# Output matmuls of each batch as narrow, wide, wide, narrow, and another order of the last two batches in a graph-attention kernel

## The chip, the cores and the metric

One core of a Trainium2 chip runs the kernel. The metric is the device time of one launch in microseconds (us); lower is better. The engines are named as the profile names them: PE (TensorE matmul) with PEld (its weight load), DVE (VectorE), ACT (ScalarE), POOL (GpSimd) and SP (SyncE, which here only issues DMAs).

## The reference

For each of 16 batches there are 512 nodes with 512 features, a condition vector and an integer label array; all is float32. The input biases that the reference draws as zeros are given small random values here.

```python
self_feat = concat(v, q) @ W_self.T + b_self           # 512 x 512 a batch
output = self_feat
for d in range(2):                                     # two edge directions
    A = adj if d == 0 else swap(adj)                   # 512 x 20 neighbours x 11 labels
    vb = A[:, :, :20] @ w_bias + b_bias
    qh, kh = self_feat @ Wq[d].T + bq[d], kv @ Wk[d].T + bk[d]     # kv: first 20 nodes; 16 heads of 32
    aff = einsum('bnhd,bmhd->bnhm', qh, kh) / sqrt(32)
    aff = where(A.sum(-1) > 0, aff, -9e15) + vb        # the same for every head
    w = softmax(aff)                                   # over the 20 neighbours
    output += per-head projection of (w @ kv) + bout[d]
return v + relu(output)
```

## The kernel before

The features lie on partitions (four groups of 128), the 512 nodes of a batch along the free axis. After a setup stage that folds the weights, 16 batches run in a software pipeline. The order of all steps is written out by hand: the string `order` lists the steps of one period with a batch offset each, and every engine takes its instructions in that order, so an instruction whose input is late holds up all that stands behind it on its engine. One period has seven products `f1` to `f7` of the self features (`feature_product`, L286), seven products `P1` to `P7` of the scores (`score_product`, L422) and one output step, `attend` (L514). The softmax of the two directions and 16 heads is done in four units (i, l), where i is the node half within a group and l the half of the partition axis: subtract the maximum (DVE, L473), exponential (ACT, L477), sum and reciprocal (DVE, L481 and L482), multiply (POOL, L486), and transpose in 32 x 32 blocks into the tile `wt` (DVE, L492 and L493).

`attend` adds the projected neighbours to what stands in PSUM. ACT has put self feature plus bias there (`seed_out`, L505), in the banks `ps_w` (output groups 0 and 1) and `ps_e` (2 and 3). For each half c of the nodes there are two kinds of matmul, all on 32 rows of the array:

- a wide one takes a 32 x 128 weight tile and serves the last 4 neighbours of all heads: 4 a half, one for each output group q;
- a narrow one takes a 32 x 32 tile and serves the first 16 neighbours of one head: 16 a half.

Each of these is two passes in the trace (float32). Before, the order is wide c=0, wide c=1, narrow c=0, narrow c=1. After it `relu` (ACT, L532) empties the banks, `residual` (POOL, L536) adds x, and `store` (SP, L539) writes one group of 128 features.

The last batch (15) has no successor to overlap with. Its scores are four plain products (`plain_scores`, L963) in `ps_a`, `ps_u` and `ps_v`, each seeded by ACT (`seed_plain`, L952), followed by `plain_max` (DVE, L978 and L980), `plain_exp` (ACT, L984), `plain_sum` (DVE, L991 and L992), `plain_normal` (L997, on POOL, and for the last piece on DVE) and `plain_turn` (DVE, L1003 and L1004). Its output step `attend_end` (L1036) runs for c=0 in `ps_w` and `ps_e`, and for c=1 in `ps_a`, `ps_u` and `ps_v`, there in two pieces by unit. Since out = x + max(o, 0) = max(o + x, x), POOL sums self feature and x beforehand (`end_sum`, L1020), ACT seeds the banks with it (`seed_end`, L1025), and one DVE maximum with x (`end_max`, L1054) gives the result, which `end_store` (L1058) writes as four DMAs of 256 KB.

Of the kernel before, what the change touches and what calls it, by code (L numbers as in the profile page):

```python
# [13 lines left out]
P = 128  # L14
# [4 lines left out]
def gat_kernel(  # L19
# [487 lines left out]
    def attend(b):  # L507
# [10 lines left out]

        for c in range(HA):
            for q in range(HL):  # L520
                r = bass.ts(q, 32)
                mm(q, c, slice(0, P), vds[b][r, c, 1], ends[r, :, c])
        for c in range(HA):
            for e in range(HL):
                for q in range(HL):
                    r = bass.ts(q, 32)
                    mm(q, c, bass.ts(e, DH), vds[b][r, c, 0, bass.ts(e, DH)], heads[r, :, c, :, e])
# [478 lines left out]
    def end_banks(a, c):  # L1006
        if c == 0:
            return [(ps_w, ps_e)[a][:, :, :NH].rearrange("p g (x n) -> p g x n", n=32)]
        if a == 0:
            return [ps_a[:, :, :NH].rearrange("p g (x n) -> p g x n", n=32)]  # L1010
        return [t[:, :NH].rearrange("p (g x n) -> p g x n", g=1, n=32) for t in (ps_u, ps_v)]

    def end_parts(a, c, of):
        banks = end_banks(a, c)
# [7 lines left out]
    def seed_end(a, c):  # L1022
        n = a * HA + c
        for to, of in end_parts(a, c, turned(ends["sum"][:, n])):
            nc.scalar.activation(to, of, AF.Identity, bias=bo[:, n : n + 1])  # L1025

    def attend_end(c, units):
# [5 lines left out]
        def mm(q, to, lhs, rhs):  # L1033
            a, g = q // HA, q % HA
            bank = ((ps_u, ps_v)[g] if a else ps_a[:, g]) if c else (ps_w, ps_e)[a][:, g]
            nc.tensor.matmul(  # L1036
                bank[to, bass.ds(lo * P, n * P)].rearrange("p (i j n) -> p i j n", i=n, n=32),
# [11 lines left out]
    def end_max(a, c):  # L1049
        if "out" not in ends:  # L1050
            ends["out"] = load.tile([P, C, N], F32, tag="x", name="end_out", bufs=3)
        to, x = (turned(t[:, a * HA + c]) for t in (ends["out"], xs[last]))
        for (of, into), (_, of_x) in zip(end_parts(a, c, to), end_parts(a, c, x)):
            nc.vector.tensor_max(into, of, of_x)  # L1054

    def end_store(a, c, queue=nc.sync):
        n = a * HA + c
        queue.dma_start(out[last, bass.ts(n, P)], ends["out"][:, n])  # L1058

    instead = {  # L1060
        "T2": fourth_keys, "T1": lambda: full_bias(0, 0, "u1"), "T4": lambda: full_bias(1, 0, "u2"), "S1": lambda: end_sum(0),
# [3 lines left out]
    with tc.manual_schedule():  # L1065
# [33 lines left out]
        go("reluW:2 sr21:1 Lv:1 tr11:1 reluE:2 sr12:1 nm21:1 res3:2")  # L1099
# [4 lines left out]
        go("nm12:1 tr21:1 St3:2 tr12:1 res1:2 St1:2 soW:1 soE:1")  # L1104
        full_bias(0, 1, "u3")
        go("res0:2 St0:2")
        plain_max(0, 0)
        plain_exp(0, 0)
        seed_plain(0, 1)
# [99 lines left out]
```

## Time and profile before

| what | value |
|---|---|
| median of 3 runs | 557.59 us (557.59 to 558.15) |
| the profiled execution | 557.27 us, of which its span (first to last instruction) is 555.5 us |
| mean granted TensorE clock | 0.993 |
| one period of the pipeline | 28.75 us |
| first and last `attend` | at 147.1 us and 536.4 us, 15 in all |
| `attend_end` | from 543.2 us on |
| last DMA of the result is issued | at 551.15 us |

In the timelines a row has the start, the duration (for merged rows from the first start to the last end), the engine, the line, what is written and read, the shape of the weight tile (rows*columns) and of one operand, and the count; in brackets stands the idle time of the engine before the row and what ended it. A matmul's end is modelled, so times between matmuls are taken from start to start. Kernel lines in rows of before are those of the printed kernel.

### The profile page before, as it was taken

The numbers are of one execution on the slowest core, as the hardware profiler recorded it, in microseconds if no ns is written. First come the engines' busy times: TensorE is split into PE (matmuls) and PEld (weight loads), VectorE is DVE, ScalarE is ACT, GpSimd is POOL, SyncE is SP. The second block draws the span as 40 slices with busy tenths as digits, with TensorE's granted clock in tenths as the row PEclk, the third lists the DMA queues.
The fourth block names the chain that finished last, engine by engine and source line by source line (L and its number), as shares of the span: only waits on it lengthen the run. The fifth ranks groups of instructions, "written<-read, shape, count | busy, mean of one in ns | idle before, by whom it ended". The sixth has DMA issues, their size and how long they took to land.

```text
span 555.5 us, 19357 instructions
## 1 busy us (share of the span) xinstructions
PE 545.2 (98%) x8034; PEld 419.9 (76%) x8034; DVE 452.4 (81%) x726; ACT 368.8 (66%) x768; POOL 441.9 (80%) x396
## 2 busy tenths in 40 slices
PE   8999999999999999999999999999999999999994
PEld 4443446979797979797978787888888787979782
DVE  0395564699989898979898988989898989898985
ACT  1244342858686959596868686868687777866652
POOL 2235675859797979797979798988989797979695
PEclk9999999999999999999999999999999999999997
DMA  8999899996786867677686858676868676645024
GB/s 292 375 400 382 296 379 344 302 292 166 230 252 175 247 181 240 193 219 215 197 234 177 241 184 217 210 196 191 214 207 218 209 211 202 192 138 167 22 95 156
DMA packets 89336, 125.80 MB, mean 226 GB/s; under 512 B 11712, under 2 KB 56800, under 8 KB 87200
## 3 DMA queue, kind: packets, MB, share of 16 engines
q1 hardware_dynamic: 87568, 121.88, 70.6%
q0 software_dynamic: 672, 1.36, 1.0%
q8 instruction: 63, 1.03, 0.8%
q10 hardware_dynamic: 1008, 1.32, 0.7%
q14 instruction: 25, 0.20, 0.1%
HBM read 85.71 MB, written 39.19 MB: 225 GB/s over the span
## 4 chain that ended last, share of the span: by engine, by line
PE 85%; issue 4%; DMA 4%; POOL 3%; DVE 2%; SPq 1%; ACT 0%; DVEq 0%; POOLq 0%
PE ps_a L422 23%; PE ps_u L286 18%; PE ps_v L286 13%; PE ps_e L422 11%; PE ps_w L422 6%; PE ps_w L514 5%; DMA x<-in_xT 2%; PE ps_v L739 2%; DMA ws_q<-in_wsT 1%; PE ps_v L214 1%; PE ps_e L514 1%; PE ps_a L963 1%; POOL cq_d L725 1%; PE ps_u L214 1%; POOL rx L194 1%
## 5 line engine op out<-in xcount | busy, mean ns | idle before, releaser
L486 POOL TENSOR_TENSOR s<-s,sm 128x640 f32<-128x640 f32 x60 | 76.5, 1277 | 40.9 <-DVE sm L482 40.9
L343 ACT ACTIVATE prod<-adj,wb_sb 128x160 f32<-128x160 int32 x165 | 80.4, 585 | 0.3 <-DMA adj<-in_adj 0.3
L536 POOL TENSOR_TENSOR o<-o,x 128x512 f32<-128x512 f32 x60 | 77.2, 1287 | 0.0
L477 ACT ACTIVATE s<-s 128x640 f32<-128x640 f32 x60 | 42.4, 730 | 25.8 <-DVE s L473 25.8
L286 PE MATMUL ps_u<-t,ws_s 128*64 128x246 f32 x480 | 55.0, 370 | 0.0
L450 DVE TENSOR_TENSOR u<-ps_a,both 128x640 f32<-128x640 f32 x30 | 24.7, 823 | 30.1 <-PE ps_a L422 30.1
L481 DVE TENSOR_REDUCE sm<-s 128x32 f32<-128x640 f32 x60 | 47.7, 795 | 0.0
L395 POOL TENSOR_TENSOR k<-g,k 128x608 f32<-128x608 f32 x30 | 44.2, 1495 | 1.1
L405 POOL TENSOR_TENSOR s<-sf 128x512 f32<-128x512 f32 x30 | 37.8, 1280 | 7.0 <-DVE sf L316 6.1
L286 PEld LDWEIGHTS ps_u<-t,ws_s 128*64 128x64 f32 x480 | 33.9, 137 | 11.7
L492 DVE STREAM_TRANSPOSE wt<-s 128x512 f32<-128x512 f32 x60 | 41.3, 688 | 1.4 <-POOL s L486 1.3
L514 PE MATMUL ps_e<-wt,vd 32*32 32x256 f32 (+1 forms) x600 | 38.3, 388 | 0.0
L367 ACT COPY both<-add 64x160 f32<-64x160 f32 (+1 forms) x68 | 21.5, 316 | 25.2 <-DVE add L356 24.6
L514 PE MATMUL ps_w<-wt,vd 32*32 32x256 f32 (+1 forms) x600 | 38.0, 388 | 0.0
L260 POOL TENSOR_TENSOR t<-x 128x492 f32<-128x492 f32 x30 | 37.4, 1248 | 0.0
L356 DVE TENSOR_REDUCE add<-prod 128x160 f32<-128x1920 f32 (+1 forms) x17 | 34.5, 2029 | 2.6 <-POOL prod L351 2.6
L316 DVE TENSOR_TENSOR sf<-ps_v,f 128x492 f32<-128x492 f32 x45 | 30.0, 667 | 6.7 <-PE ps_v L286 5.9
L260 POOL TENSOR_TENSOR t<-x,t 128x492 f32<-128x492 f32 x30 | 34.7, 1158 | 0.2
L176 ACT ACTIVATE xn<-xn 128x512 f32<-128x512 f32 x56 | 34.5, 617 | 0.0
L422 PEld LDWEIGHTS ps_a<-g,sf 128*64 128x64 f32 x480 | 30.3, 137 | 5.6 <-issue 5.4
L348 DVE TENSOR_REDUCE cond<-adj 128x160 f32<-128x1760 int32 (+1 forms) x17 | 31.1, 1829 | 4.0 <-DMA adj<-in_adj 4.0
L422 PE MATMUL ps_a<-g,sf 128*64 128x152 f32 x480 | 34.2, 295 | 0.0
(329 smaller groups left out, 1511.4 us busy)
## 6 DMA issues: line engine op xcount, KB each, us to landing
g<-g_d SPq DMA_DIRECT2D x60, 304.0 KB, 4.8
g_d<-st SPq DMA_DIRECT2D x16, 1064.0 KB, 6.2
out_T<-o SPq DMA_DIRECT2D x60, 256.0 KB, 4.4
xn<-in_xn SPq DMA_DIRECT2D x28, 512.0 KB, 5.9
x<-in_xT SPq DMA_DIRECT2D x28, 512.0 KB, 7.2
adj<-in_adj SPq DMA_DIRECT2D x32, 440.0 KB, 4.7
vd<-bd_d SPq DMA_DIRECT2D x64, 64.0 KB, 2.0
nz<-nz_d SPq DMA_DIRECT2D x14, 256.0 KB, 7.0
```

What stands on the lines that cost most here:

```text
L260: nc.gpsimd.tensor_sub(t, one, two)
L286: nc.tensor.matmul(to[bass.ts(a, RA), bass.ts(i, HN)], lhs, x[:, k], start=(n, i, k) == (1, 0, 0), stop=k == 1, skip_group_check=True,)
L343: nc.scalar.activation(label_sums(b)[:, :, l], labels(b)[:, :, l], AF.Copy, scale=wb_sb[:, l : l + 1])
L395: op(t, one(), two())
L405: op(t, one(), two())
L422: nc.tensor.matmul(to[bass.ts(a, RA), j, :, 1:], rows[:, k, bass.ts(j, RA)], keys[:, k, a].rearrange("p (x m) -> p x m", m=ND), start=Fals ...
L477: nc.scalar.activation(t, t, AF.Exp)
L481: nc.vector.tensor_reduce(sm, rows_of(b, i, l), AX.X, ALU.add)
L486: nc.gpsimd.tensor_mul(t, t, us.pop((b, "sum", i, l)).unsqueeze(2).to_broadcast([P, 32, NG]))
L492: nc.vector.transpose(wts[b][:, i, l, : W * 4 // 5], t[:, :, :MW])
L514: nc.tensor.matmul((ps_w, ps_e)[a][to, g, bass.ts(c, NH)].rearrange("p (i j n) -> p i j n", i=2, n=32), lhs, rhs, start=False, stop=True, ...
L536: nc.gpsimd.tensor_add(t, t, xs[b][:, c])
```

## The change

It has two parts.

**The order within `attend`.** The narrow matmuls of c=0 now come first, then the wide ones of both halves, then the narrow ones of c=1. The matmuls are the same.

```diff
+        def head_run(c):
+            for e in range(HL):
+                for q in range(HL):
+                    r = bass.ts(q, 32)
+                    mm(q, c, bass.ts(e, DH), vds[b][r, c, 0, bass.ts(e, DH)], heads[r, :, c, :, e])
+
+        head_run(0)
         for c in range(HA):
             for q in range(HL):
                 r = bass.ts(q, 32)
                 mm(q, c, slice(0, P), vds[b][r, c, 1], ends[r, :, c])
-        for c in range(HA):
-            for e in range(HL):
...
+        head_run(1)
```

**The last two batches.** The last three sums of batch 14 are taken before its transposes (`sr12` ahead of `tr11`), so that POOL's last two multiplications of batch 14 stand ahead of the residual additions of batch 13. Of the four `end_sum`s two go (n = 0 and 2): `seed_end` for c=0 takes the self feature alone, and x is added at the end, for output groups 0 and 1 by ACT's relu and a POOL addition (`end_relu`, `end_add`), for groups 2 and 3 by DVE in one instruction (`end_both`). Batch 14's group with a=1, c=0 also gets relu and x in one DVE step (`out_both`). The last piece of `plain_normal` moves from DVE to POOL. The first unit of `attend_end` for c=1 is written to `ps_w` and `ps_e`, so that `ps_a`, `ps_u` and `ps_v` hold the last unit alone: 128 columns a group in place of 256. The result of the last batch leaves in six DMAs: two of 256 KB and four of 128 KB, one of the small ones last.

```diff
-    def end_banks(a, c):
+    def end_banks(a, c, i):
         if c == 0:
             return [(ps_w, ps_e)[a][:, :, :NH].rearrange("p g (x n) -> p g x n", n=32)]
+        if i == 0:
+            return [(ps_w, ps_e)[a][:, :, bass.ds(NH, P)].rearrange("p g (x n) -> p g x n", n=32)]
         if a == 0:
-            return [ps_a[:, :, :NH].rearrange("p g (x n) -> p g x n", n=32)]
...
+            return [ps_a[:, :, :P].rearrange("p g (x n) -> p g x n", n=32)]
...
+    def rectified(to, of, x):
+        for g in range(HA):
+            nc.vector.scalar_tensor_tensor(to[:, g], of[:, g], 0.0, x[:, g], ALU.max, ALU.add)
...
-        go("reluW:2 sr21:1 Lv:1 tr11:1 reluE:2 sr12:1 nm21:1 res3:2")
+        go("reluW:2 sr21:1 Lv:1 sr12:1 reluE:2 nm21:1 tr11:1")
...
-        go("nm12:1 tr21:1 St3:2 tr12:1 res1:2 St1:2 soW:1 soE:1")
+        go("nm12:1 tr21:1 tr12:1")
         full_bias(0, 1, "u3")
-        go("res0:2 St0:2")
+        go("res3:2 St3:2 soW:1 soE:1 res1:2 St1:2 res0:2 St0:2")
         plain_max(0, 0)
+        seed_plain(0, 1)
         plain_exp(0, 0)
-        seed_plain(0, 1)
...
-        plain_normal(1, 1, second, nc.vector)
+        plain_normal(1, 1, second)
         plain_turn(1, 1, second)
-        go("res1:1 St1:1 res2:1 St2:1 res3:1 St3:1")
-        attend_end(1, (0,))
         attend_end(1, (1,))
-        for c in range(HA):
-            for a in range(HA):
-                end_max(a, c)
-                end_store(a, c, nc.sync if (a, c) == (1, 1) else nc.scalar)
+        end_relu()
+        end_add()
+        for a in range(HA):
+            end_max(a, 0)
+        end_both()
+        for a in range(HA):
+            end_max(a, 1)
...
+        end_store(1, 1, bass.ts(1, NH), nc.sync)
```

How it stands on the engines, in three places. First PE, one batch's `attend` between a feature product (L286) and a score product (L422); `wt` are the transposed softmax weights, `vd` the projected neighbours; before, the wide rows (128 output partitions) and the first narrow ones:

```order
L286 MATMUL ps_v<-x_1530,ws_s 64x246 x8
L514 MATMUL ps_w<-wt_1610,vd_1699 128x256 x2
L514 MATMUL ps_e<-wt_1610,vd_1699 128x256 x2
L514 MATMUL ps_w<-wt_1610,vd_1699 128x256 x2
L514 MATMUL ps_e<-wt_1610,vd_1699 128x256 x2
L514 MATMUL ps_w<-wt_1610,vd_1699 32x256 x2
L514 MATMUL ps_e<-wt_1610,vd_1699 32x256 x2
```

After, from the last narrow rows of c=0 to the first ones of c=1:

```order
L514 MATMUL ps_w<-wt_1610,vd_1699 32x256 x2
L514 MATMUL ps_e<-wt_1610,vd_1699 32x256 x2
L514 MATMUL ps_w<-wt_1610,vd_1699 128x256 x2
L514 MATMUL ps_e<-wt_1610,vd_1699 128x256 x2
L514 MATMUL ps_w<-wt_1610,vd_1699 128x256 x2
L514 MATMUL ps_e<-wt_1610,vd_1699 128x256 x2
L514 MATMUL ps_w<-wt_1610,vd_1699 32x256 x2
L514 MATMUL ps_e<-wt_1610,vd_1699 32x256 x2
```

Before, the 32 narrow matmuls stand in one run behind the wide ones; after, 16 stand ahead of the wide ones and 16 behind. The array changes its tile shape four times a batch, with the way in and out, where it changed it three times.

Second POOL, from the multiplications of batch 14 (L486, tiles `s` and `sm`) to the first ones of batch 15 (`last`); `o` and `x_5619` are batch 13's result and input. Before:

```order
L486 TENSOR_TENSOR s_11_6668<-s_11_6668,sm_11_6757 128x640
L1020 TENSOR_TENSOR end_sum<-sf_6666,x_6367 128x512
L486 TENSOR_TENSOR s_10_6705<-s_10_6705,sm_10_6826 128x640
L536 TENSOR_TENSOR o_1_6836<-o_1_6836,x_5619 128x512
L486 TENSOR_TENSOR s_01_6728<-s_01_6728,sm_01_6839 128x640
L536 TENSOR_TENSOR o_0_6823<-o_0_6823,x_5619 128x512
L949 TENSOR_TENSOR full_6922<-cq_6502,both_6707 128x640
L536 TENSOR_TENSOR o_0_6823<-o_0_6823,x_5619 128x512
L997 TENSOR_TENSOR last_6926<-last_6926,max_6927 128x640
```

After:

```order
L486 TENSOR_TENSOR s_11_6668<-s_11_6668,sm_11_6757 128x640
L1027 TENSOR_TENSOR end_sum<-sf_6666,x_6367 128x512 x2
L486 TENSOR_TENSOR s_10_6705<-s_10_6705,sm_10_6827 128x640
L486 TENSOR_TENSOR s_01_6728<-s_01_6728,sm_01_6835 128x640
L952 TENSOR_TENSOR full_6915<-cq_6502,both_6707 128x640
L539 TENSOR_TENSOR o_1_6838<-o_1_6838,x_5619 128x512
L539 TENSOR_TENSOR o_0_6824<-o_0_6824,x_5619 128x512 x2
L1000 TENSOR_TENSOR last_6927<-last_6927,max_6928 128x640
```

No addition of batch 13 stands between batch 14's last two multiplications any more, and a second `end_sum` stands ahead of them.

Third DVE, the end of the program, from the last reciprocal of the softmax (`max` holds the sums by then) on. Before:

```order
L992 RECIPROCAL max_7087<-max_7087 128x16
L1003 STREAM_TRANSPOSE wt_6980<-last_7086 128x256
L1004 STREAM_TRANSPOSE wt_6980<-last_7086 128x64
L997 TENSOR_TENSOR last_7086<-last_7086,max_7087 128x320
L1003 STREAM_TRANSPOSE wt_6980<-last_7086 128x256
L1004 STREAM_TRANSPOSE wt_6980<-last_7086 128x64
L1054 TENSOR_TENSOR end_out<-ps_w,x_6367 128x2x8x32
L1054 TENSOR_TENSOR end_out<-ps_e,x_6367 128x2x8x32
L1054 TENSOR_TENSOR end_out<-ps_a,x_6367 128x2x8x32
L1054 TENSOR_TENSOR end_out<-ps_u,x_6367 128x8x32
L1054 TENSOR_TENSOR end_out<-ps_v,x_6367 128x8x32
```

After:

```order
L995 RECIPROCAL max_7090<-max_7090 128x16
L1006 STREAM_TRANSPOSE wt_6977<-last_7089 128x256
L1007 STREAM_TRANSPOSE wt_6977<-last_7089 128x64
L1006 STREAM_TRANSPOSE wt_6977<-last_7089 128x256
L1007 STREAM_TRANSPOSE wt_6977<-last_7089 128x64
L1072 TENSOR_TENSOR end_out<-ps_w,x_6367 128x2x4x32
L1072 TENSOR_TENSOR end_out<-ps_e,x_6367 128x2x4x32
L1063 SCALAR_TENSOR_TENSOR end_out<-ps_e,x_6367 128x8x32 x2
L1072 TENSOR_TENSOR end_out<-ps_a,x_6367 128x2x4x32
L1072 TENSOR_TENSOR end_out<-ps_u,x_6367 128x4x32
L1072 TENSOR_TENSOR end_out<-ps_v,x_6367 128x4x32
```

The multiplication L997 is gone from DVE, and the three steps that read the banks of the last matmuls have half their columns.

More of the change, by code (lines that the diff above doesn't have):

```diff
@@ L522, in attend @@
                 mm(q, c, slice(0, P), vds[b][r, c, 1], ends[r, :, c])
-        for c in range(HA):
-            for e in range(HL):
-                for q in range(HL):
-                    r = bass.ts(q, 32)
-                    mm(q, c, bass.ts(e, DH), vds[b][r, c, 0, bass.ts(e, DH)], heads[r, :, c, :, e])
+        head_run(1)
     def relu(b, a):
@@ L1020, in end_sum, with seed_end @@
         nc.gpsimd.tensor_add(ends["sum"][:, n], sfs[last][:, n], xs[last][:, n])
-    def seed_end(a, c):
+    def seed_end(a, c, i=0):
         n = a * HA + c
-        for to, of in end_parts(a, c, turned(ends["sum"][:, n])):
+        for to, of in end_parts(a, c, i, ends["sum"] if c else sfs[last]):
             nc.scalar.activation(to, of, AF.Identity, bias=bo[:, n : n + 1])
@@ L1034, in mm @@
             a, g = q // HA, q % HA
-            bank = ((ps_u, ps_v)[g] if a else ps_a[:, g]) if c else (ps_w, ps_e)[a][:, g]
+            bank = ((ps_u, ps_v)[g] if a else ps_a[:, g]) if lo else (ps_w, ps_e)[a][:, g]
             nc.tensor.matmul(
-                bank[to, bass.ds(lo * P, n * P)].rearrange("p (i j n) -> p i j n", i=n, n=32),
+                bank[to, bass.ds(NH * (c - lo), n * P)].rearrange("p (i j n) -> p i j n", i=n, n=32),
                 lhs, rhs, start=False, stop=True, skip_group_check=True,
@@ L1103, in gat_kernel @@
         plain_scores(1, 0)
-        go("nm12:1 tr21:1 St3:2 tr12:1 res1:2 St1:2 soW:1 soE:1")
+        go("nm12:1 tr21:1 tr12:1")
         full_bias(0, 1, "u3")
-        go("res0:2 St0:2")
+        go("res3:2 St3:2 soW:1 soE:1 res1:2 St1:2 res0:2 St0:2")
         plain_max(0, 0)
+        seed_plain(0, 1)
         plain_exp(0, 0)
-        seed_plain(0, 1)
+        plain_max(1, 0, first)
         plain_sum(0, 0)
         plain_normal(0, 0)
+        plain_max(1, 0, second)
+        plain_exp(1, 0)
+        plain_scores(0, 1)
         full_bias(1, 1, "u1")
-        go("res2:2 St2:2")
-        plain_max(1, 0, first)
-        plain_max(1, 0, second)
-        plain_scores(0, 1)
-        plain_exp(1, 0)
-        seed_plain(1, 1, first)
-        seed_plain(1, 1, second)
         plain_turn(0, 0)
@@ L1122, in gat_kernel @@
         plain_normal(1, 0)
-        end_sum(2)
-        end_sum(1)
+        go("res2:2 St2:2")
+        seed_plain(1, 1, first)
+        seed_plain(1, 1, second)
         go("OUT:1 Lv:0")
```

75 lines of the change are left out of this document (55 added, 20 removed).

## The prediction

> **What bounds the kernel now.** I read the page first, for the busy shares and the chain that ended last, then a table by stage over one period, then PE's timeline, then all engines at the end.
>
> ```profile
> span 555.5 us, 19357 instructions
> PE 545.2 (98%) x8034; PEld 419.9 (76%) x8034; DVE 452.4 (81%) x726; ACT 368.8 (66%) x768; POOL 441.9 (80%) x396
> PE 85%; issue 4%; DMA 4%; POOL 3%; DVE 2%; SPq 1%; ACT 0%; DVEq 0%; POOLq 0%
> ```
>
> PE is busy for 98% of the span, and 85% of the chain that ended last is PE's. A share of the span hides stages, so here is one period of the pipeline (columns: time, then busy time of PE, PEld, DVE, ACT, POOL):
>
> ```profile
> 437.19:465.94 28.75, 28.75 (x418) 23.93 (x420) 25.46 (x40) 22.00 (x46) 25.59 (x23) 1.00 0.73 210
> ```
>
> In the steady state PE never stops, at full clock (1.00), and DVE and POOL have more than 3 us of 28.75 to spare. A microsecond that PE saves in a period is a microsecond of the kernel. This is PE's timeline through one output step, starts in the first column:
>
> ```profile
> 319.62 0.48 PE L514 MATMUL ps_w<-wt,vd 32*128 32x256 f32 x2
> ...
> 319.94 0.38 PE L514 MATMUL ps_w<-wt,vd 32*128 32x256 f32 x2
> ...
> 320.37 0.38 PE L514 MATMUL ps_w<-wt,vd 32*128 32x256 f32 x2
> ...
> 320.69 0.41 PE L514 MATMUL ps_w<-wt,vd 32*32 32x256 f32 x2
> ...
> 320.93 0.38 PE L514 MATMUL ps_w<-wt,vd 32*32 32x256 f32 x2
> ...
> 321.15 0.59 PE L514 MATMUL ps_w<-wt,vd 32*32 32x256 f32 x2
> 321.36 0.40 PE L514 MATMUL ps_e<-wt,vd 32*32 32x256 f32 x1
> ...
> 321.80 0.39 PE L514 MATMUL ps_e<-wt,vd 32*32 32x256 f32 x2
> 322.12 2.29 PE L422 MATMUL ps_a<-g,sf 128*64 128x152 f32 x32
> ```
>
> The step takes 319.62 to 322.12, 2.50 us. The four wide passes start at 319.62, 319.94, and then two more up to 320.37: 0.32 for the first, some 0.21 each after it. The narrow ones of c=0 begin at 320.69 and run their second pass from 320.93. The narrow ones of c=1 should then begin at 321.15, all 16 within 0.1 us, as those of c=0 did. Only two do. The next starts at 321.36, a whole pass later, and the last at 321.80. This is the flaw that the first part of the change touches: a narrow run straight behind another narrow run loses time, with no change of tile shape between them.
>
> **Part one, the order in `attend`.** What single blocks cost stands in the last batch's own output step, where one wide and one narrow half follow each other and then a wide one:
>
> ```profile
> 543.22 0.48 PE L1036 MATMUL ps_w<-wt,vd 32*128 32x256 f32 x2
> ...
> 543.86 0.40 PE L1036 MATMUL ps_w<-wt,vd 32*32 32x256 f32 x2
> ...
> 544.52 0.49 PE L1036 MATMUL ps_a<-wt,vd 32*128 32x128 f32 x4
> ```
>
> A narrow block of one half, with the change of shape behind it, takes 543.86 to 544.52, 0.66 us. In the step above the two wide halves take 319.62 to 320.69, 1.07, and the two narrow halves 320.69 to 322.12, 1.43. Two single narrow blocks would take 1.32. So the new order is 0.66 + 1.07 + 0.66 = 2.39 against 2.50: 0.11 less a batch, although it pays one more change of shape, which the 0.66 holds. What no row shows is a narrow block straight behind 128*64 tiles, and the wide halves behind a narrow block. I take the same prices; the bounds are 0.1 better a batch (a first wide pass at 0.21 in place of 0.32) and 0.34 worse. The 0.34 is the loss itself: a second half inside one shape should add two passes, 0.43 by the wide ones from 319.94 to 320.37, to the 0.66, which makes 1.09, and it took 1.43. `attend` runs 15 times, each on PE's chain: 15 x 0.11 = 1.65 us. Its first matmuls need the same as before, the seeds of c=0 in both banks and `vd`, so nothing is waited for earlier.
>
> The Trainium skill, TensorEngine Tiling (Array Packing), section Tiling Modes, Key Properties, says that changing the tiling mode drains the array, and changing only the tile does not. That speaks against this change: four drains in place of three. By that rule alone, with 0.32 less 0.21 for a drain, the step would be some 0.11 longer, not shorter; with the end as worked out below the time would be 556.6. The trace agrees that each change of shape costs (0.32 from the last wide pass to the narrow ones); no run here shows yet whether it costs more than the loss.
>
> **Part two, the end.** Four stretches change. First, before the last batch's third score product:
>
> ```profile
> 524.47 1.28 POOL L486 TENSOR_TENSOR s<-s,sm 128x640 f32<-128x640 f32 x1 [1.38 <-DVE sm L482]
> 525.71 1.29 POOL L536 TENSOR_TENSOR o<-o,x 128x512 f32<-128x512 f32 x1
> 526.94 1.28 POOL L486 TENSOR_TENSOR s<-s,sm 128x640 f32<-128x640 f32 x1
> ...
> 527.56 2.24 PE L963 MATMUL ps_u<-g,sf 128*64 128x152 f32 x32
> ...
> 528.26 0.71 DVE L492 STREAM_TRANSPOSE wt<-s 128x512 f32<-128x512 f32 x1 [1.33 <-POOL s L486]
> ...
> 529.62 2.24 PE L963 MATMUL ps_v<-g,sf 128*64 128x152 f32 x32
> ...
> 532.15 0.74 PE L963 MATMUL ps_a<-k_last,sf 128*64 128x152 f32 x8 [0.29 <-ACT ps_a L952]
> ```
>
> POOL adds a residual (525.71) ahead of the multiplication that DVE waits for 1.33 us; behind that on DVE's queue stands `plain_max`, on whose result ACT's copy waits, and on the copy PE at 532.15. From 527.56 to 529.62 such a product takes 2.06, so PE was free at 531.68 and lost 0.47 (0.29 of it shown as idle, since the end of a row is modelled). With the residual moved back the chain comes 1.2 us earlier, PE's input at about 530.95, 0.7 before PE is free: the wait goes, and nothing else is late there. The second `end_sum` lies in POOL's 1.38 of idle time and takes a further 1.28 of it, just hidden; without that cover it would delay the transposes by its excess, at most 0.1. The stores of batch 13 move behind POOL's later additions on SP's queue; ahead of the `vd` loads of batch 15 stands, as before, the store of `res2`, which POOL ends about as early against PE as before, so those loads keep their place.
>
> Second, from the last score product to the last transposes:
>
> ```profile
> 546.44 1.04 DVE L997 TENSOR_TENSOR last<-last,max 128x320 f32<-128x320 f32 x1
> 547.51 0.45 DVE L1003 STREAM_TRANSPOSE wt<-last 128x256 f32<-128x256 f32 x1
> ```
>
> and on POOL
>
> ```profile
> 545.18 0.73 POOL L997 TENSOR_TENSOR last<-last,max 128x320 f32<-128x320 f32 x1 [0.85 <-DVE max L992]
> ```
>
> The second multiplication cost DVE 1.04 and stood between its transposes. On POOL it follows the first: 545.18 + 0.73 + 0.73 = 546.64; 0.04 to DVE, as from 528.22 to 528.26 above, and from there 0.63 to PE, as from 547.51 to 548.14 below: 547.31 in place of 548.14. That is 0.83 less, if POOL is free at 545.18. It idled 0.85 before that; between its two multiplications stand two additions as before (a residual for an `end_sum`), but the one ahead of them starts later behind another residual, and I estimate that 0.3 of the 0.85 is left. If POOL came late, the gain would shrink by as much.
>
> Third and fourth, the last matmuls, the maximum and the store:
>
> ```profile
> 548.14 0.58 PE L1036 MATMUL ps_a<-wt,vd 32*128 32x128 f32 x2 [1.55 <-DVE wt L1004]
> 549.76 0.69 DVE L1054 TENSOR_TENSOR end_out<-ps_a,x 128x512 f32<-128x512 f32 x1 [0.51 <-PE ps_v L1036]
> 550.70 0.41 DVE L1054 TENSOR_TENSOR end_out<-ps_v,x 128x256 f32<-128x256 f32 x1
> 551.15 0.33 SPq L1058 DMA_DIRECT2D out_T<-end_out  x1
> ```
>
> and from the page's list of DMA issues (size, us to landing)
>
> ```profile
> vd<-bd_d SPq DMA_DIRECT2D x64, 64.0 KB, 2.0
> out_T<-end_out SPq DMA_DIRECT2D x1, 256.0 KB, 3.5
> ```
>
> The matmuls themselves keep their 1.62 (548.14 to 549.76). DVE's other four steps of the end, about 0.41 each, fit beside them. Behind them stood 549.76 to 551.11, 1.35; with half the columns one step of 0.41 and two smaller ones, estimated at 0.2 to 0.3 each, are some 0.85: 0.5 less (0.25 to 0.7). ACT's relu and POOL's 1.3 us addition for the other groups, with their store, end before. The last store has 128 KB, which no row shows; between 2.0 for 64 KB and 3.5 for 256 KB I take 2.7, 0.8 less (0 to 1.5). What lies behind the landing (551.15 + 3.5 to 555.5, 0.85) stays.
>
> The Trainium skill, DMA: Bandwidth & Descriptors, section Anatomy of one DMA, has a fixed 2.0 us plus bytes over 436 GB/s, fitted on the GpSimd path. By that, 128 KB less saves an estimated 0.3 us, and the sum below would be 0.5 smaller.
>
> **The sum.** 1.65 + 0.47 + 0.83 + 0.5 + 0.8 = 4.25 us, of which 2.60 at the end. The profiled execution took 557.27 (555.5 of span and 1.77 around it), so 553.0; it lies 0.32 under the median of the runs shown, so 553.3 for a median. A measurement of this kernel can tell about 0.2%, 1.1 us.
>
> **The rivals.**
>
> *The second narrow block keeps its loss.* If the 0.34 is not due to the block before it being narrow but to its tiles having been used in this step, it is paid again: 2.39 + 0.34 = 2.73, 0.23 more than before, 15 times 3.45; with 2.60 gained at the end the time is 0.85 above before, 558.4, no change that can be told. For it: the two blocks use the same 16 tiles. Against it: the two that start on time at 321.15 do so when c=0's last pass ends, and the rest a pass later, which looks like a queue held up by work in progress, and the wide block empties it. The Trainium skill, TensorEngine Tiling (Array Packing), section Tiling Modes, would send the time the same way, through the drain.
>
> *Both narrow blocks pay, and it is slower.* In the trace a narrow block starts smoothly only behind a wide one. Behind 128*64 tiles it might lose the 0.34 as well: 3.07 a step, 0.57 more than before, 15 times 8.6 less 2.60: 563.5. It decides from a step of 2.75 on. Against it: the wide block, which follows 128*64 tiles in the kernel before, shows no such loss there, only 0.11 in its first pass.
>
> *The order in `attend` gives nothing* (2.50 as before): 557.59 - 2.60 = 555.0.
>
> *The end gives only the 0.47*, because the store takes its 3.5 and POOL's chain of additions holds up its multiplications: 1.65 + 0.47, 555.5. For it: POOL's margins at the end are 0.1 to 0.3 us.
>
> **How the numbers follow.** Forecast 0.72, with its own range 551.8 to 554.9 (down: the store and the maximum at their better ends, 0.9, and 0.04 a step of the possible 0.1, 0.6; up: the store at 3.5 and half of the gain in `attend` gone, 1.6). Second block keeps its loss 0.08; both pay 0.05; nothing in `attend` 0.07; little at the end 0.08. Faster is the forecast and the last two: 0.87; same 0.08; slower 0.05. The range takes in the last two and their errors: 551.8 to 556.0. That the change does not do what it says is no rival: the engines' order shows the blocks and the moved steps.
>
> **What would show it.** Right: a period of 28.64; in a step narrow rows first, their second pass 0.24 later, wide rows 0.66 after the start, narrow again at 1.73, and L422 at 2.39; no narrow pair with 0.59. PE without the wait of 0.29 at the third score product; two POOL multiplications back to back at the end; the last DVE step of 128 columns, and the last store landing in under 3 us. Wrong: a period of 28.75 or more, a narrow block whose starts spread over 0.4 us, or a last store that takes 3.5.

## The result, and the profile after

The changed kernel takes 553.28 us (median of 10 runs, 552.74 to 556.81) against 557.88 us (median of 10 runs, 557.24 to 558.70) for the kernel before in the same comparison: ratio of the times (after over before) 0.9925, 95% interval 0.9909 to 0.9942. That is 4.6 us less by the medians and 4.2 by the ratio (3.2 to 5.1), where 4.25 were forecast. The profiled execution is one of 553.24 us. Three lines of its page, span, busy times and the chain that ended last:

```profile
span 551.5 us, 19357 instructions
...
PE 542.3 (98%) x8034; PEld 414.7 (75%) x8034; DVE 451.7 (82%) x729; ACT 369.5 (67%) x770; POOL 439.7 (80%) x395
...
PE 91%; DMA 4%; POOL 2%; DVE 1%; issue 1%; SPq 0%; ACT 0%; DVEq 0%; POOLq 0%
```

PE has lost 2.9 us of busy time, and its share of the chain has grown from 85% to 91%: less of the chain is now waiting at the end. PE's timeline through one output step of the changed kernel, and the start of the next batch's (start, duration):

```profile
319.34 0.41 PE L514 MATMUL ps_w<-wt,vd 32*32 32x256 f32 x2
...
319.58 0.38 PE L514 MATMUL ps_w<-wt,vd 32*32 32x256 f32 x2
...
319.98 0.48 PE L514 MATMUL ps_w<-wt,vd 32*128 32x256 f32 x2
...
321.07 0.41 PE L514 MATMUL ps_w<-wt,vd 32*32 32x256 f32 x2
...
321.72 0.74 PE L422 MATMUL ps_a<-g,sf 128*64 128x152 f32 x8
347.97 0.41 PE L514 MATMUL ps_w<-wt,vd 32*32 32x256 f32 x2
```

The blocks take 0.64 (319.34 to 319.98), 1.09 (to 321.07) and 0.65 (to 321.72), together 2.38; the period is 28.63 (to 347.97). All 15 steps are 2.38 long, to 0.01, where they were 2.50. Next, the third score product of the last batch: PE's row of the second product, its row of the third, and POOL's two multiplications in one row:

```profile
528.39 2.24 PE L966 MATMUL ps_v<-g,sf 128*64 128x152 f32 x32
530.45 0.69 PE L966 MATMUL ps_a<-k_last,sf 128*64 128x152 f32 x8
523.36 2.50 POOL L486 TENSOR_TENSOR s<-s,sm 128x640 f32<-128x640 f32 x2 [0.15 <-DVE sm L482]
```

The third follows the second after 2.06 us, without a wait. The end, on POOL, DVE and PE:

```profile
543.31 1.41 POOL L1000 TENSOR_TENSOR last<-last,max 128x320 f32<-128x320 f32 x2 [0.20 <-DVE max L995]
545.12 0.20 DVE L1007 STREAM_TRANSPOSE wt<-last 128x64 f32<-128x64 f32 x1
545.47 0.38 PE L1043 MATMUL ps_a<-wt,vd 32*128 32x128 f32 x2 [1.59 <-DVE wt L1007]
545.25 0.39 DVE L1072 TENSOR_TENSOR end_out<-ps_w,x 128x256 f32<-128x256 f32 x1
...
545.89 0.74 DVE L1063 SCALAR_TENSOR_TENSOR end_out<-ps_e,x 128x256 f32<-128x256 f32 x2
546.56 0.42 DVE L1072 TENSOR_TENSOR end_out<-ps_a,x 128x256 f32<-128x256 f32 x1
...
547.10 0.28 DVE L1072 TENSOR_TENSOR end_out<-ps_v,x 128x128 f32<-128x128 f32 x1
547.41 0.33 SPq L1084 DMA_DIRECT2D out_T<-end_out  x1
```

DVE no longer idles 0.51 us for PE's last matmuls; `ps_a` follows 1.09 us behind their start (545.47 to 546.56), where it was 1.62. The end's stores, size and us to landing:

```profile
out_T<-end_out SPq DMA_DIRECT2D x3, 128.0 KB, 2.5
out_T<-end_out ACTq DMA_DIRECT2D x1, 256.0 KB, 2.4
out_T<-end_out SPq DMA_DIRECT2D x1, 256.0 KB, 2.6
out_T<-end_out ACTq DMA_DIRECT2D x1, 128.0 KB, 2.8
```

Here a store's size does not order its time: 256 KB landed in 2.4 and 2.6 us, 128 KB in 1.7 to 2.8 (2.5 is the median of three on SP). That was the first sign that one price of the prediction stood on a wrong reason.

One table on the end of all kernels, counted from the start of batch 14's output step (the second-last), so that scatter in the setup drops out; landing and clock come from the trace's semaphore and clock records:

| kernel | batch 14's step starts | DVE ends | last store issued | landed | span ends |
|---|---|---|---|---|---|
| before | 536.43 | +14.69 | +14.72 | +18.17 | +19.07 |
| after | 534.69 | +12.69 | +12.72 | +15.49 | +16.77 |
| order alone | 534.78 | +14.57 | +14.59 | +18.06 | +18.95 |
| end alone | 535.51 | +12.82 | +12.84 | +15.53 | +16.81 |
| four stores | 534.77 | +12.69 | +12.72 | +16.13 | +17.03 |
| before, gap filled | 538.19 | +14.15 | +14.18 | +18.10 | +18.99 |
| before, multiplication on POOL | 537.31 | +13.79 | +14.27 | +17.89 | +18.80 |
| after, late stores | 537.18 | +12.81 | +13.26 | +16.41 | +17.69 |
| after, shared end | 535.31 | +12.75 | +12.77 | +15.79 | +16.71 |

How far one profiled execution can be trusted: the three kernels with another order in `attend` (below) have the end of the changed kernel, and without their longer step their spans end at 16.76, 16.72 and 16.50, for 16.77 here. Their last store landed 2.77, 2.72 and 2.27 us after its issue, for 2.77.

### The profile page after: what moved, and what is told of

Read it like the earlier page. It is cut to its first block, busy times and chain, and to the rows that moved or that the text cites. A ratio compares the mean times of both kernels' runs of the same rounds, so it can differ in the third digit from the quotient of the medians.

```text
span 551.5 us, 19357 instructions
## 1 busy us (share of the span) xinstructions
PE 542.3 (98%) x8034; PEld 414.7 (75%) x8034; DVE 451.7 (82%) x729; ACT 369.5 (67%) x770; POOL 439.7 (80%) x395
## 4 chain that ended last, share of the span: by engine, by line
PE 91%; DMA 4%; POOL 2%; DVE 1%; issue 1%; SPq 0%; ACT 0%; DVEq 0%; POOLq 0%
PE ps_a L422 23%; PE ps_u L286 18%; PE ps_v L286 14%; PE ps_e L422 11%; PE ps_w L422 6%; PE ps_w L514 6%; PE ps_k L678 2%; PE ps_v L742 2%; PE ps_a L966 2%; DMA ws_q<-in_wsT 1%; PE ps_v L214 1%; DMA cq_d<-c 1%; PE ps_e L514 1%; DMA g_d<-st 1%; PE ps_u L678 1%; PE ps_v L678 1%
## 5 line engine op out<-in xcount | busy, mean ns | idle before, releaser
L486 POOL TENSOR_TENSOR s<-s,sm 128x640 f32<-128x640 f32 x60 | 76.3, 1274 | 38.4 <-DVE sm L482 38.4
L539 POOL TENSOR_TENSOR o<-o,x 128x512 f32<-128x512 f32 x59 | 75.2, 1277 | 0.8 <-ACT o L1098 0.8
L286 PE MATMUL ps_u<-t,ws_s 128*64 128x246 f32 x480 | 55.0, 370 | 0.0
L286 PEld LDWEIGHTS ps_u<-t,ws_s 128*64 128x64 f32 x480 | 33.9, 137 | 11.7
L514 PE MATMUL ps_e<-wt,vd 32*32 32x256 f32 (+1 forms) x600 | 36.6, 389 | 0.0
L514 PE MATMUL ps_w<-wt,vd 32*32 32x256 f32 (+1 forms) x600 | 36.6, 389 | 0.0
L422 PEld LDWEIGHTS ps_a<-g,sf 128*64 128x64 f32 x480 | 30.3, 137 | 5.6 <-issue 5.4
L422 PE MATMUL ps_a<-g,sf 128*64 128x152 f32 x480 | 34.2, 295 | 0.0
```

The source lines that it names most:

```text
L286: nc.tensor.matmul(to[bass.ts(a, RA), bass.ts(i, HN)], lhs, x[:, k], start=(n, i, k) == (1, 0, 0), stop=k == 1, skip_group_check=True,)
L422: nc.tensor.matmul(to[bass.ts(a, RA), j, :, 1:], rows[:, k, bass.ts(j, RA)], keys[:, k, a].rearrange("p (x m) -> p x m", m=ND), start=Fals ...
L486: nc.gpsimd.tensor_mul(t, t, us.pop((b, "sum", i, l)).unsqueeze(2).to_broadcast([P, 32, NG]))
L514: nc.tensor.matmul((ps_w, ps_e)[a][to, g, bass.ts(c, NH)].rearrange("p (i j n) -> p i j n", i=2, n=32), lhs, rhs, start=False, stop=True, ...
L539: nc.gpsimd.tensor_add(t, t, xs[b][:, c])
```

## The experiments

### Each part alone

The new `attend` in the kernel before:

```diff
+        head_run(0)
         for c in range(HA):
             for q in range(HL):
                 r = bass.ts(q, 32)
                 mm(q, c, slice(0, P), vds[b][r, c, 1], ends[r, :, c])
-        for c in range(HA):
...
+        head_run(1)
```

> The kernel before with the new order in attend alone; the end of the program is as before. Theory (two narrow runs one behind the other lose 0.34 us, whatever stands at the end): attend 2.38 us instead of 2.50 in all 15 batches, 15 x 0.12 = 1.8 us earlier at the last batch. To this comes a second theory on the clock: the granted clock of PE falls on a fixed grid (547.98 us in before, 548.08 in after), and in before the last matmuls (from 548.14) lay behind that point. Moved forward by 1.8 us they lie ahead of it and take about 1.1 us instead of 1.62: 0.5 us more, so 2.3 us faster, about 555.6. Rival: the end is bound by DVE and the clock does not matter: 1.8 us faster, 556.1. Rival: the order gives nothing without the new end: 557.9.

Measured: 555.99 us, ratio 0.9966 (0.9954 to 0.9979), and 2.38 us a step in 15 steps. The end is that of before to 0.01 us, less the 0.12 of batch 14's step (18.95 for 19.07). So the order is worth its 1.8 us alone. The clock's second gain did not come: the clock fell here at 545.72, and the last matmuls, from 546.37, ran at half clock (columns: stretch, its length, busy PE, PEld, DVE, ACT, POOL, granted clock, DMA share, GB/s).

```profile
546.30:548.00 1.70, 1.48 (x40) 0.81 (x40) 1.20 (x4) 0.00 (x0) 1.70 (x2) 0.50 0.56 211
```

I had taken the point at which it falls as fixed at 548. The full-clock stretch begins at another phase in each execution (5.26 us in before, 6.42 here) and lasted 542.719 us there and 539.306 here, 159 and 158 times 3.413.

The old `attend` in the changed kernel:

```diff
-        head_run(0)
         for c in range(HA):
             for q in range(HL):
                 r = bass.ts(q, 32)
                 mm(q, c, slice(0, P), vds[b][r, c, 1], ends[r, :, c])
+        head_run(0)
         head_run(1)
```

> The changed kernel with the old order in attend (wide, wide, narrow, narrow). Theory: attend is 2.50 us again and the program 1.8 us longer than the changed kernel, with its end as there (31.5 us from the start of the second-last output step to the end of the span, less than 34.6 in before): about 555.1, 2.8 us faster than before. With the clock grid: the last matmuls begin at 547.2 or 547.3, ahead of the grid point at about 548.0, and are mostly at full clock, so at most 0.2 longer. If the two edits were independent, this and the run with the order alone would add up to the whole change, 4.6 us; by the clock theory the two add up to 5.0 or 5.1, since each alone brings the last matmuls ahead of the grid point. Rival: the end gives only the 0.5 us of the score product's wait: 557.4.

Measured: 554.48 us, ratio 0.9945 (0.9931 to 0.9958), 2.50 a step, and an end of 16.81 (16.77 after, 0.12 of which is the step). The two parts add up as far as these runs can tell: 1.9 and 3.1 us by the ratios, 5.0 together against 4.2 for the whole, each to within some 0.7; whether a part of the gain counts twice, as the clock theory has it, cannot be read from that.

### Why two narrow runs lose time

Three other orders in the changed kernel, each timed once; the step's length is from the trace. `end_run(c)` is the wide half c. Wide and narrow in turn:

```diff
-        head_run(0)
-        for c in range(HA):
...
-        head_run(1)
+        for c in range(HA):
+            end_run(c)
+            head_run(c)
```

> The changed kernel with attend as wide c=0, narrow c=0, wide c=1, narrow c=1: no two narrow runs are neighbours, with two changes of shape more than in the old order. Theory (only a narrow run straight behind a narrow run loses 0.34 us; a wide half with its change of shape costs 0.64 and a narrow half with its own 0.66 to 0.69): 2.60 to 2.66 us a batch, 0.22 to 0.28 more than the changed kernel's 2.38 and more than the old order's 2.50, so 3.3 to 4.2 us longer in all. Rival (the second narrow run of a step loses 0.34 whatever stands between): 2.94 to 3.0.

Measured: 2.61 us in all 15 steps (556.90 us in all). The first rows of the four blocks and of what follows:

```profile
320.95 0.48 PE L514 MATMUL ps_w<-wt,vd 32*128 32x256 f32 x2
...
321.59 0.41 PE L514 MATMUL ps_w<-wt,vd 32*32 32x256 f32 x2
...
322.25 0.48 PE L514 MATMUL ps_w<-wt,vd 32*128 32x256 f32 x2
...
322.90 0.40 PE L514 MATMUL ps_w<-wt,vd 32*32 32x256 f32 x2
...
323.56 0.48 PE L422 MATMUL ps_a<-g,sf 128*64 128x152 f32 x4
```

The second narrow run (322.90 to 323.56) costs no more than the first (321.59 to 322.25), 0.66, though it uses the same 16 tiles, so the loss is not in their second use; one change of shape more than in the changed kernel costs 0.23. The narrow runs ahead:

```diff
-        head_run(0)
-        for c in range(HA):
...
-        head_run(1)
+        head_run(0)
+        head_run(1)
+        end_run(0)
+        end_run(1)
```

> The changed kernel with attend as narrow c=0, narrow c=1, wide c=0, wide c=1: the two narrow runs are neighbours again, but stand ahead of the wide ones; as many changes of shape as in the changed kernel's order less one. Theory (neighbours lose 0.34): 1.43 + 1.07 = 2.50 us a batch, as in the old order, 1.8 us longer in all than the changed kernel. Rival (the loss belongs to narrow runs behind wide ones, or to the place at the end of the step): 2.16, 3.3 us shorter than the changed kernel. Rival (a narrow run behind 128*64 tiles pays as well): 2.6 or more.

Measured: 2.50 us in all 15 (554.44 us in all). The pair loses as much at the front as at the back: the neighbour decides, not the place. The old order with the second run's tiles reversed:

```diff
-            for e in range(HL):
-                for q in range(HL):
+            for e in range(HL)[:: 1 - 2 * c]:
+                for q in range(HL)[:: 1 - 2 * c]:
                     r = bass.ts(q, 32)
                     mm(q, c, bass.ts(e, DH), vds[b][r, c, 0, bass.ts(e, DH)], heads[r, :, c, :, e])
```

> The changed kernel with the old order in attend (wide, wide, narrow c=0, narrow c=1), where the 16 tiles of the second narrow run are taken in the reverse order. Theory (PE's queue is in order: the second run's first matmul waits until its own 32x32 tile is free, and those behind it wait with it; in reverse it asks first for the tile that comes free last): the loss grows by the 0.09 us between the first and the last start of a narrow pass, 2.55 to 2.65 us a batch. Rival (a fixed price of a second narrow run, whichever tile it begins with): 2.50 as in the old order. Rival (the loss comes from taking the same tile again too soon, and a reverse order helps the later ones): under 2.45.

Measured: 2.50 us in all 15 (556.29 us in all). This went against my theory: the second run comes as late as in the normal order. The first fence is PE's row of the kernel before at which the run goes on, the second the start of the step and that row with the tiles reversed; both lie 1.74 us after the step's start (319.62 and 321.59):

```profile
321.36 0.40 PE L514 MATMUL ps_e<-wt,vd 32*32 32x256 f32 x1
```

```profile
321.59 0.48 PE L514 MATMUL ps_w<-wt,vd 32*128 32x256 f32 x2
...
323.33 0.41 PE L514 MATMUL ps_w<-wt,vd 32*32 32x256 f32 x2
```

So it does not wait for its own first tile. The weight loads of the kernel before show where it stands still:

```profile
320.93 0.50 PEld L514 LDWEIGHTS ps_w<-wt,vd 32*32 32x32 f32 x3
321.35 0.10 PEld L514 LDWEIGHTS ps_e<-wt,vd 32*32 32x32 f32 x1
```

Only three loads lie in the half microsecond from 320.93, when the first run's second pass begins; the others come from 321.35 on, when that pass is over. From its start to the next run of starts it is 0.43 (320.93 to 321.36); at a change of shape in the changed kernel 0.40 (319.58 to 319.98), and between the passes of one run 0.24. A second narrow run thus stops PE about as a change of shape does, and its starts then come less densely (14 of them in 0.20, from 321.36 on, where the first run's 16 took 0.12, from 320.69 on). The prediction read the row at 321.15 as two matmuls that start on time; its 0.59, for the 0.37 that one takes there, tells that it merges two, and the second starts at 321.34. What holds the loads back stayed open.

### The clock at the end

The kernel before with PE kept busy ahead of its last matmuls:

```diff
         attend_end(1, (0,))
+        for _ in range(12):
+            none = zero.bitcast(mybir.dt.bfloat16)[:32, :P]
+            nc.tensor.matmul(
+                ps_w[:, 0, NH:].rearrange("p (x n) -> p x n", n=P), none,
+                none.unsqueeze(1).to_broadcast([32, NH // P, P]), start=False, stop=True, skip_group_check=True,
+            )
         attend_end(1, (1,))
```

> The kernel before with twelve small matmuls of zero weights (32 rows, 256 columns, bf16) in PE's idle 1.55 us ahead of the last output matmuls; they add zeros to part of a bank that nothing reads any more. Theory (PE's idle time lets the granted clock fall at a grid point just ahead of the last matmuls): with PE busy the clock stays up to the next grid point 3.4 us later, the last matmuls take about 1.1 us instead of 1.62, and the end comes 0.5 us earlier: 557.4. Rival 1: the clock falls all the same, or DVE bounds the stretch: no change, 557.9. Rival 2: the filling runs over the start of the last matmuls: some 0.1 to 0.3 us later.

Measured: 559.12 us, ratio 1.0023 (1.0011 to 1.0035), slower; but its setup ended 1.77 us later in the profile (from an `x` load that was issued 1.4 us later, at 114 us, far ahead of the edit), and why the timed runs are longer was not settled. The end can be compared by itself. There the matmuls ran at full clock:

```profile
549.90:551.00 1.10, 0.95 (x40) 0.56 (x40) 1.10 (x3) 0.00 (x0) 1.10 (x2) 1.00 0.53 197
```

```profile
550.40 0.68 DVE L1054 TENSOR_TENSOR end_out<-ps_e,x 128x512 f32<-128x512 f32 x1
551.00 0.68 DVE L1054 TENSOR_TENSOR end_out<-ps_a,x 128x512 f32<-128x512 f32 x1
```

`ps_a` follows 1.10 us after their start instead of 1.62, DVE has no wait left and ends 0.54 earlier (14.15 for 14.69). So the clock theory holds for the matmuls. But the store landed only 0.07 earlier: it took 3.9 us instead of 3.5. DVE's gain did not reach the end.

### What a store's time is made of

Four whole stores at the end of the changed kernel:

```diff
-        end_store(0, 1, bass.ts(0, NH), nc.sync)
         end_store(0, 0, slice(0, N), nc.scalar)
-        end_store(1, 1, bass.ts(0, NH), nc.sync)
         end_store(1, 0, slice(0, N), nc.sync)
-        end_store(0, 1, bass.ts(1, NH), nc.scalar)
-        end_store(1, 1, bass.ts(1, NH), nc.sync)
+        end_store(0, 1, slice(0, N), nc.scalar)
+        end_store(1, 1, slice(0, N), nc.sync)
```

> The changed kernel with four whole stores of 256 KB at the end instead of two whole and four halves. Theory 1 (a store's time comes from what else is in flight, not from its size): the last store lands 2.4 to 2.9 us after its issue, as the halves did (2.77). Theory 2 (the order in which SP checks the DMA semaphores at the end): with two DMAs fewer the last store has the semaphore that is checked last, so that the span ends 0.90 us after the landing, as in before, instead of 1.28. Together: the span is 0.3 to 0.6 us shorter than the changed kernel's. Rival, the price in the prediction (3.5 us for 256 KB, 2.7 for 128 KB): lands 3.4 to 3.5 us after its issue, and the span is 0.3 us longer or, if the semaphores' order does not matter either, 0.7 us.

Measured: 553.61 us, ratio 0.9923 (0.9911 to 0.9936), the same as the changed kernel. The last store landed after 3.4 us, the rival's figure (15 of its 16 parts after 2.76, one 0.65 later), and the span ended 0.91 us behind it instead of 1.28, so the second theory holds. On the first the run does not decide: by its last part it speaks for a price by size, by the other 15 (2.4 to 2.9 expected) for what is in flight. Two others speak against a price by size. The kernel before with one edit:

```diff
-        plain_normal(1, 1, second, nc.vector)
+        plain_normal(1, 1, second)
```

> The kernel before with one edit: the second multiplication of the last score product on GpSimd, straight behind the first, instead of on DVE. Theory 1 (the terms of the prediction add up): PE's last matmuls begin 0.83 us earlier and the end comes 0.83 us earlier, or up to 1.3 if they also escape the clock's fall: 556.6 to 557.1. Theory 2 (the end of the kernel before is bound by its stores: six of 256 KB are issued in its last 2.6 us, at about 366 GB/s, and 950 KB are still to be moved when the last one is issued): the three additions of batch 14 on GpSimd and their stores come 0.73 later, so that as much is left to move; DVE ends 0.8 to 1.3 us earlier, but the last store is issued behind batch 14's at about 550.9 and lands at most 0.4 us earlier: 557.5 to 558.0, no change that can be told.

Measured: 557.57 us, ratio 0.9993 (0.9983 to 1.0003): nothing that can be told, as the second theory says. DVE ended 0.90 earlier (13.79 for 14.69), where the prediction prices 0.83, and the last store landed only 0.28 earlier. From 549.7 us on the DMA engines were full, here and in the kernel before (here first):

```profile
549.70:552.20 2.50, 0.00 (x0) 0.00 (x0) 1.35 (x3) 0.00 (x0) 1.43 (x2) 0.50 1.03 383
552.20:554.40 2.20, 0.00 (x0) 0.00 (x0) 0.00 (x0) 0.00 (x0) 0.00 (x0) 0.50 1.00 374
```

```profile
549.70:551.80 2.10, 0.00 (x0) 0.00 (x0) 1.35 (x3) 0.00 (x0) 0.13 (x1) 0.50 1.03 381
551.80:553.80 2.00, 0.00 (x0) 0.00 (x0) 0.00 (x0) 0.00 (x0) 0.00 (x0) 0.50 0.93 345
```

And the changed kernel with its own end stores, where three of batch 14's come late (`late(queue, c)` stores its chunk c):

```diff
-        go("res1:1 St1:1 St2:1 res3:1 St3:1")
+        go("res1:1 res3:1")
...
         end_relu()
+        late(nc.scalar, 2)
+        late(nc.scalar, 3)
...
         end_store(0, 1, bass.ts(0, NH), nc.sync)
+        late(nc.sync, 1)
```

> The changed kernel with three of the four stores of the second-last batch (256 KB each) issued later, two on ACT behind its last relu (from 544.7 us) and one on SP behind the first of the end's stores (at about 546.1), with the data, the order on DVE, GpSimd and PE, and the last store of 128 KB as they are. Theory 1 (the end is a queue of transfers at about 366 GB/s; the time of the last store is what is still to be moved when it is issued): 1.79 MB are to be moved from about 545.6 on, 4.9 us, so the last store lands at about 550.5 to 550.9 instead of 550.2, 3.3 us or more after its issue although it has 128 KB, and the span is 0.5 to 0.9 us longer. Theory 2 (a store's time goes by its own size, the price in the prediction): 2.7 to 2.8 us after its issue, no change.

Measured: 556.64 us (a single time; its setup ended 2.5 us later than the changed kernel's). The end is 0.92 us longer (17.69 for 16.77): 0.54 because SP got to the last store later, 0.38 because the same 128 KB took longer:

```profile
out_T<-end_out SPq DMA_DIRECT2D x1, 128.0 KB, 3.1
```

With more to be moved at the same time, 128 KB take 3.1 instead of 2.8; the direction is that of the first theory, the size less than its 3.3 or more. The next run shows the other end, 128 KB in 1.7 and 256 KB in 2.0 where little else was under way. Taken together, a store's time follows what is in flight beside it; the size alone, 0.3 us for 128 KB there, is the smaller part.

### What the multiplication cost on DVE

The changed kernel with the second multiplication on DVE and nothing on POOL beside it:

```diff
-        plain_normal(1, 1, second)
+        plain_normal(1, 1, second, nc.vector)
...
-        nc.gpsimd.tensor_add(t, t, xs[last][:, 0])
+        nc.vector.tensor_add(t, t, xs[last][:, 0])
...
         end_relu()
-        end_add()
...
         end_store(0, 1, bass.ts(0, NH), nc.sync)
+        end_add()
         end_store(0, 0, slice(0, N), nc.scalar)
```

> The changed kernel with the second multiplication of the last score product on DVE again, as in the kernel before, but with GpSimd idle beside it: the last group's addition of x, which would run there on GpSimd, is done by DVE at the very end (0.6 to 1.3 us later stores of that group). Theory (the 1.04 us that this 128x320 multiplication took on DVE in the kernel before came from GpSimd's addition running beside it): 0.45 to 0.55 us with GpSimd idle, so that DVE's last transposes end at most 0.1 us later than in the changed kernel. Rival (the multiplication with its broadcast operand costs DVE 1.04 by itself): 1.04, and PE's last matmuls begin 0.5 to 0.6 us later than in the changed kernel, counted from the end of the last score product.

Measured: 554.31 us (a single time). The multiplication took 0.45:

```profile
544.53 0.45 DVE L1000 TENSOR_TENSOR last<-last,max 128x320 f32<-128x320 f32 x1
```

```profile
out_T<-end_out SPq DMA_DIRECT2D x3, 128.0 KB, 1.7
out_T<-end_out SPq DMA_DIRECT2D x1, 256.0 KB, 2.0
```

In the kernel before it took 1.04, and the first of POOL's three additions in this row ran beside it, from 545.86 for some 1.27 us:

```profile
545.86 3.96 POOL L536 TENSOR_TENSOR o<-o,x 128x512 f32<-128x512 f32 x3
```

DVE began at 546.44 and ended at 547.48, 0.35 after that addition. The Trainium skill, SBUF — State Buffer, section Who interferes with whom, says that a DVE instruction with two inputs in SBUF contends with a GpSimd instruction that reads SBUF, and that the later one is blocked until the other ends; the trace agrees, since what is left behind the addition, 0.35, is no more than the 0.45 that the multiplication takes alone. My bound of 0.1 us for DVE's last transposes was too small: they ended 0.3 later than in the changed kernel, since the multiplication stands between them.

### A version made from the findings

DVE's first step at the end goes to ACT and POOL, and two DMAs fewer put the last store's counter last:

```diff
-        for a in range(HA):
-            end_max(a, 0)
+        end_max(1, 0)
...
-        t = end_out()[:, 0]
-        nc.gpsimd.tensor_add(t, t, xs[last][:, 0])
+        for c, at in ((0, slice(0, N)), (1, bass.ts(0, NH))):
+            t = end_out()[:, c, at]
+            nc.gpsimd.tensor_add(t, t, xs[last][:, c, at])
...
-        go("res1:1 St1:1 St2:1 res3:1 St3:1")
+        go("res1:1 St1:1 res3:1")
+        store_pair(last - 1, 1)
```

> The changed kernel with three edits at the end that the runs so far point to: the group's first half in ps_w (c=1) is finished by ACT's relu and GpSimd's addition instead of by DVE, which is the engine that ends last (one step of 0.31 us less on it); that group is stored whole, by ACT; and two stores of the second-last batch are one of 512 KB, so that with two DMAs fewer the last store has the semaphore that is checked last at the end of the program. Theory: DVE's last step ends 0.2 to 0.3 us earlier, bound then by PE's last matmuls; the last store lands 0.1 to 0.3 us earlier, since some 1 MB has to be moved from 545.7 on in any case; and the span ends 0.9 us behind it instead of 1.28. In all 0.5 to 0.7 us less than the changed kernel: 552.6 to 552.8, about 0.1%, at the edge of what can be told; the trace shows the parts. Rival (GpSimd's second addition ends late, at 546.7 or more, and the store that waits for it becomes the last one): no gain over the changed kernel, 553.3.

Measured: 553.27 us, ratio 0.9915 (0.9902 to 0.9929): no gain over the changed kernel that can be told. The span ends 0.91 behind the landing, as expected, but DVE is no earlier:

```profile
547.24 0.42 DVE L1072 TENSOR_TENSOR end_out<-ps_a,x 128x256 f32<-128x256 f32 x1 [0.32 <-issue]
```

It waits 0.32 where its step was taken away: PE's last matmuls, begun at 546.09, are done 1.15 later. PE and DVE end together in the changed kernel, and I had counted only DVE. The store's last part came 0.58 us behind the other 15, which ate most of the 0.38.

## Why the prediction was right, and where it was not

**`attend`: right.** 15 x 0.12 = 1.8 us measured, 15 x 0.11 forecast. The prices of the blocks held (0.64, 1.09, 0.65 for 0.66, 1.07, 0.66), behind 128*64 tiles too. The rivals (the second narrow block keeps its loss; both pay; the order gives nothing) fell in the changed kernel, in the run with wide and narrow in turn and in that with the order alone. The rule that a change of tiling mode drains the array (the Trainium skill, TensorEngine Tiling (Array Packing), Tiling Modes) is borne out in the price (0.23 for one more) but would have given the wrong sign here, since a second run of 16 tiles loses 0.34 without a change.

**The third score product: right.** The output steps of batches 13 and 14 are 14.93 apart instead of 15.56; without the 0.12 of the step that is 0.51 less, 0.47 forecast.

**The second multiplication: right on PE, for a reason half seen.** From the last score product's end to PE's last matmuls it took 4.80 before (543.34 to 548.14) and 3.97 after (541.50 to 545.47), 0.83 less as forecast; POOL was free in time. That DVE's 1.04 was mostly waiting for POOL showed only in the run without POOL beside it.

**The last maximum: mis-sized, 0.97 for 0.5.** From the last transposes' end to DVE's end it took 3.03 (548.08 to 551.11) and takes 2.06 (545.32 to 547.38). The half columns were priced rightly: DVE's last three steps took 0.82 (546.56 to 547.38), 0.85 forecast. The step that failed is "The matmuls themselves keep their 1.62": at full clock they take 1.09. The trace of before had the reason, had I asked for the granted clock in that stretch, 0.50; here it is for before and, behind it, for after, 1.00:

```profile
548.10:549.80 1.70, 1.49 (x40) 0.81 (x40) 1.19 (x3) 0.00 (x0) 1.70 (x2) 0.50 0.57 214
```

```profile
545.40:546.60 1.20, 0.94 (x40) 0.58 (x40) 1.20 (x5) 0.00 (x0) 0.64 (x1) 1.00 0.06 22
```

PE's idle 1.55 us let the clock fall at a point of a grid of 3.413 us, whose phase is another in each execution; in the profiled execution after, the points fell beside the matmuls, and that is luck: with the multiplication on DVE one fell at 545.91, 0.18 us behind the start of the last matmuls, and `ps_a` followed 1.51 us behind that start:

```profile
547.24 0.42 DVE L1072 TENSOR_TENSOR end_out<-ps_a,x 128x256 f32<-128x256 f32 x1 [0.35 <-PE ps_v L1043]
```

So some 0.4 of the 0.97 hangs on the phase.

The Trainium skill, TensorE: Matmul & The Clock Gate, Part 1, gives a free-running window of 3413 ns; the lengths above agree. It has the clock fall after an idle window. Here it fell 0.9 us into an idle time with the order alone (PE idle from about 544.8, fall at 545.72) and 0.55 into one with the multiplication moved alone (547.46, 548.01), but not at the changed kernel's point 544.67, 0.78 into one, nor at 125.30 in the setup of the run with late stores, 1.9 into one. So the length of the idle time does not tell whether the clock falls; what decides stayed open.

**The last store: 0.8 forecast, 0.31 measured, and the step failed in its reason.** Landing came 0.68 sooner (3.45 to 2.77 after the issue), near the 0.8; 0.35 of it are the first 15 of the store's 16 parts (2.92 to 2.57), 0.33 the last part's lag behind them, whose cause is open. With the changed end the landing took 2.27 to 2.77 in five profiled executions. But "between 2.0 for 64 KB and 3.5 for 256 KB" took a time for a price of size. Six stores of 256 KB were issued in the last 2.6 us before; the engines were full for 4 us at 345 to 381 GB/s, and the last store took 1.4 us more than the 2.0 of 256 KB with little in flight: that queue, and 0.53 of lag of its last part. And 0.38 was given back: "What lies behind the landing (551.15 + 3.5 to 555.5, 0.85) stays" is wrong. At its end the program has SP check eight DMA counters one after the other, by the trace's events some 0.06 each. The last store's counter was the eighth, and is the second since there are two DMAs more: 1.28 us from landing to end instead of 0.90. The 0.3 that the prediction worked out from the Trainium skill (DMA: Bandwidth & Descriptors, Anatomy of one DMA: a fixed time plus bytes) meets the net 0.31 by chance: the landing moved by 0.68, and the rest is the order of the checks.

**What the sum did not hold.** The terms at the end do not stand each for itself. The multiplication alone, priced 0.83, gave the kernel before 0.28 at the landing, and full clock alone 0.07, because the stores of batch 14, issued among those of the end, kept the DMA engines full. In the changed kernel the last of these is issued at 543.24 and lands 2.3 later, about when the end's first is issued (545.66). The prediction gives no term to batch 14's additions and stores, which the change moves ahead; by these runs it is probably this move that lets the other terms reach the end: taken back in part, with the late stores, the span was 0.92 longer (0.54 of it SP's order, 0.38 the last store). No run makes the move alone in the kernel before. The total was close because two errors nearly cancelled: 0.5 too little for the maximum, 0.5 too much for the store. In the profiles: 1.8 + 0.51 + 0.83 + 0.97 + 0.31 = 4.4, less 0.44 by which the setup of the profiled execution ended later (its first step at 147.55 for 147.11) is 4.0, and the spans differ by 4.0.

## What to carry to other kernels

Price blocks of small tiles by what stands next to them: two dense runs of 32x32 tiles in a row cost more here (0.34 us) than an added change of shape between them (0.23), and the rows of the first start after each block show it. At a program's end, add up the bytes that are still to be moved before pricing a single last store: if the DMA engines are full, earlier arithmetic buys little until earlier stores have left (here 0.07 and 0.28 us for 0.54 and 0.90). Ask for the granted clock in every short stretch behind an idle PE, the end above all.

## What the hardware did that I had not expected

- A second narrow run stops PE for 0.43 us from the last pass's start, a change of shape for 0.40; reversing its tiles changed nothing (2.50 both).
- Half clock came at points of a 3.413 us grid whose phase changes with each execution, after 0.55 us of idle PE in one and not after 0.78 or 1.9 in others.
- The end of the program costs 0.90 us behind the last landing when the last store's counter is the last checked and 1.28 when it is the second (0.89 to 0.91 in six profiled executions, 1.28 in six, and 1.38 in the one where a store of ACT's landed last).
- One of a store's 16 parts can land up to 0.65 us after the other 15 (0.53 before, 0.20 after, 0.58 with the shared end). What delays it stayed open.
- The setup's end varies by more than 3 us between profiled executions (the first step's start at 146.70 to 150.05), which is why the ends were compared from batch 14's step.
